# A graph layer with gathered edges: a memset of 128x320 floats on GpSimd in place of the no-operation between gathers

## The chip, the cores and the metric

The kernel runs on one core of one Trainium2 chip. The metric is the device time of one execution in microseconds (us), lower is better. The time before is the median of three runs.

## The reference

A graph has 12500 nodes with 128 features each (`x`, float32) and 412500 directed edges (`src`, `dst`), sorted by destination. Each edge has a gate, a number between 0 and 1, computed from the difference of its two nodes, and the gated differences are summed at the destination:

```python
theta = x[dst] - x[src]
w = sigmoid(relu(theta @ W1 + b1) @ W2 + b2)
agg = segment_sum(w * theta, dst)
indeg = segment_sum(ones, dst)
out = layernorm(x + agg + indeg * (x @ W4 + b4))
```

W1 and W4 are 128x128, W2 is 128x1. Everything is float32.

## The kernel before

**Tables.** `theta @ W1` is the difference of two rows of `x @ W1`, so the kernel first builds a table `z` in DRAM with one row of 256 floats (1 KB) per node: `x @ W1` with the bias, and `x` itself. An edge then needs one row of `z` for its source.

**Parts and blocks.** The edges are cut into 302 parts (`NS`), each for a run of destinations; two parts make a block of at most 96 destinations, 151 blocks in all. The first 26 parts (`PLAIN`) hold 1024 edges and run while the tables and lists are prepared; they are the early parts. Each later part holds up to 1402 edges: 1024 whose source rows are gathered from DRAM, and up to 384 "hot" ones whose source rows TensorE picks out of tables in SBUF, by one-hot matrices (`hot_tiles` on ScalarE, L996 and L998, `hot_products`, L1010, and `hot_rows`, L1051 to L1058, on TensorE).

**The gathers.** `gather(s)` issues the gathers of part `s` on GpSimd: eight indirect DMAs (four for the last part), each of which fetches 128 rows of 1 KB into one of the eight slots of a buffer of `zbuf`; seven such buffers go round. Line L373 is the gather. Ahead of every gather but the very first stands a GpSimd no-operation, `rest` (L367). Manual dependences without semaphores keep the order gather, no-operation, gather. There are 2204 gathers in the later parts, 208 in the early ones.

**What sets the order.** The order of the instructions on TensorE (PE), VectorE (DVE) and ScalarE (ACT) is written out by hand in `part(s)`. For one later part it is about this:

- `logits(s)` on DVE: subtract the gathered half-rows from the products of the destinations `y` (L908), relu times W2 (L913), sum over features (L919); one-hot matrices of the destinations (L888);
- `spread_ahead(s)`: issue the gathers of part `s + 3`. The first of them waits for one semaphore: `paced[s + 3]`, the newest product of `hot_products` or `hot_rows` on PE at that time. The other seven wait for nothing but the order on GpSimd (and for their buffer to be free);
- `add_block` (PE, L1101) sums the weighted rows of the block before; `spread_pair` (PE, L878) and `hot_rows` prepare the next block;
- `open_gate` (ACT, L925) turns the sums into gates; `hot_logits` (DVE, L1068) does the same as `logits` for the hot edges of a block; `weigh` (DVE, L953) and `weigh_rest` (ACT, L960) multiply four of the eight slots each by their gates;
- `normalize` (DVE, L1174 to L1199) is the layernorm of a finished block, whose result goes out by DMA.

`place`, spread over the parts in small steps, prepares the lists of edges for later parts (DVE, L485 to L653; L548 is one of its larger instructions). The core's SyncE (SP) issues most of the plain DMAs.

So GpSimd works a little ahead of the loop of the other engines: the rows of part `s + 3` are asked for while part `s` runs, and how far it runs ahead is bounded by the paced product. The pacing and the call in `spread_ahead` are these lines:

```python
if PLAIN + AHEAD <= s + 3 < NS:
    if s >= PLAIN + 4:
        paced[s + 3] = newest[0]
    gather(s + 3)
```

Of the kernel before, what the change touches and what calls it, by code (L numbers as in the profile page):

```python
# [9 lines left out]
F32 = mybir.dt.float32  # L10
# [10 lines left out]
P = 128  # L21
# [21 lines left out]
PLAIN = FIRST + MORE  # L43
# [36 lines left out]
def gnn_resnorm(  # L80
# [37 lines left out]
    nc = tc.nc  # L118
# [21 lines left out]
    const = ctx.enter_context(tc.tile_pool(name="const", bufs=1))  # L140
# [15 lines left out]
    def set_of(s):  # L156

        s0 = 0 if s < PLAIN else PLAIN + (s - PLAIN) // S2 * S2
        return placed[s0], s - s0
# [42 lines left out]
    def early(n, dtype=F32):  # L202

        a = used_of[0]
        used_of[0] = a + -(-n // (2 if dtype == BF16 else 1))
        assert used_of[0] <= HR * HT * D
        t = tabs_flat[:, a:used_of[0]]
        return t if dtype == F32 else t.bitcast(dtype)
# [49 lines left out]
    rest = early(D)  # L258
# [83 lines left out]
    def slots(s):  # L342
        return [h * J + j for h in range(2) for j in range(pairs(s))]
# [7 lines left out]
    def rows_of(s):  # L351

        if s < NH:
            t = zbuf[s // 2].rearrange("p k d -> p (k d)")[:, (s % 2) * BE:(s % 2 + 1) * BE]
            return t.rearrange("p (k d) -> p k d", d=D)
        return zbuf[(s - NH + NX) % NZ]

    gathers = []
    table_steps = []
    paced = {}  # L360

    def gather(s):

        (src_i, _, _), i = set_of(s)
        for k in slots(s):
            if gathers:
                rest = nc.gpsimd.engine_nop()  # L367
                tc.add_manual_dep(
                    rest.ins, gathers[-1].ins.name,
                    mybir.DependencyInfo(mybir.DependencyClass.NoSync, mybir.DependencyReason.DATA),  # L370
                    reason="between two gathers")
                gathers.append(rest)
            ins = nc.gpsimd.indirect_dma_start(  # L373
                out=rows_of(s)[:, k, :], out_offset=None, in_=z if s >= NH else x,
                in_offset=IndirectOffsetOnAxis(ap=src_i[:, k, i:i + 1], axis=0))
            waits = [(gathers[-1], mybir.DependencyClass.NoSync)] if gathers else []
            at = (s * K + k) * 4 * len(chunks) // (NH * K) - 6
            if s < NH and 0 <= at < len(table_steps):
                waits.append((table_steps[at], mybir.DependencyClass.Sync))
            if k == 0 and s in paced:  # L380
                waits.append((paced[s], mybir.DependencyClass.Sync))
            for other, kind in waits:
                tc.add_manual_dep(
                    ins.ins, other.ins.name,
                    mybir.DependencyInfo(kind, mybir.DependencyReason.DATA), reason="gathers' pace")
            gathers.append(ins)
# [300 lines left out]
    with tc.manual_schedule(engines={SP}), tc.tile_pool(name="work", bufs=2) as wp, tc.tile_pool(  # L687
        name="ps_y", bufs=2, space=bass.MemoryType.PSUM
    ) as ps_y, tc.tile_pool(
        name="ps_l", bufs=1, space=bass.MemoryType.PSUM  # L690
# [526 lines left out]
        def gather_first():  # L1217

            while gathered[0] < AHEAD and (gathered[0] + 1) * len(chunks) <= (len(done) + 1) * NH:
                gather(gathered[0])  # L1220
                gathered[0] += 1
# [70 lines left out]
        def early_part(s):  # L1292
# [15 lines left out]
            if h == 0:  # L1308
# [3 lines left out]
                if b:  # L1312
                    load_u(b - 1)
            gather(s + AHEAD)
            one_hot_w(s)
            logits(s)
# [39 lines left out]
        def spread_ahead(s):  # L1356
# [5 lines that stand above are left out]
# [269 lines left out]
```

## Time and profile before

| | us |
|---|---|
| runs | 3891.53, 3894.61, 3896.5 |
| median of the runs | 3894.61 |
| profiled execution, its own time | 3877.69 |
| its span in the trace | 3875.8 |
| granted TensorE clock, mean of the span | 0.800 |

The profiled execution is 16.9 us (0.4%) under the median of the runs; the prediction starts from its span and says how it stands to the median. The span starts with the tables: in its first tenth the DMAs move up to 265 GB/s in a slice. From about 560 us on to 3838 us the later parts run in the same way, at some 113 GB/s.

How to read the views: a row of a timeline has the start in us, the duration, the engine, the line, the operation, the tile written and the tile read, and in brackets the idle time of the engine ahead of it with what released it. A row of a group has the count, the busy time, the mean in ns and the idle time ahead of its instructions with the releasers. "issue" is idle time in which the engine waited for nothing that the profile shows, "remote" a wait whose releaser the profile cannot name. No-operations are not shown in any view; they lie in the gaps.

### The profile page before, as it was taken

The numbers are of one execution on the slowest core, as the hardware profiler recorded it, in microseconds if no ns is written. First come the engines' busy times: TensorE is split into PE (matmuls) and PEld (weight loads), VectorE is DVE, ScalarE is ACT, GpSimd is POOL, SyncE is SP. The second block draws the span as 40 slices with busy tenths as digits, with TensorE's granted clock in tenths as the row PEclk, the third lists the DMA queues.
The fourth block names the chain that finished last, engine by engine and source line by source line (L and its number), as shares of the span: only waits on it lengthen the run. The fifth ranks groups of instructions, "written<-read, shape, count | busy, mean of one in ns | idle before, by whom it ended". The sixth has DMA issues, their size and how long they took to land.

```text
span 3875.8 us, 56094 instructions
## 1 busy us (share of the span) xinstructions
PE 2445.5 (63%) x15792; PEld 2080.0 (54%) x15792; DVE 2570.0 (66%) x5694; ACT 2136.0 (55%) x5542; POOL 2324.0 (60%) x2421
## 2 busy tenths in 40 slices
PE   6776566666666666666666666656666666666666
PEld 5555455555555555555555555555555555555555
DVE  6445257777775777777657777776577777765555
ACT  5454455555556555555555555555555555555554
POOL 5544436666666666666666666666666666666663
PEclk9786777778778787878888888788878887788887
DMA  7332224444444444444444434444444444444432
GB/s 265 116 106 76 76 76 112 113 110 115 112 113 120 113 113 113 114 112 112 113 119 113 113 112 111 114 111 112 113 113 112 114 113 114 112 112 112 113 108 71
DMA packets 259988, 437.36 MB, mean 113 GB/s; under 512 B 69817, under 2 KB 177800, under 8 KB 258132
## 3 DMA queue, kind: packets, MB, share of 16 engines
q0 software_dynamic: 114752, 312.11, 28.9%
q1 hardware_dynamic: 142946, 115.19, 11.0%
q10 hardware_dynamic: 1970, 6.40, 0.5%
q8 instruction: 127, 2.08, 0.2%
q14 instruction: 193, 1.58, 0.1%
HBM read 406.12 MB, written 27.33 MB: 112 GB/s over the span
## 4 chain that ended last, share of the span: by engine, by line
DVE 29%; another core or an unknown queue 23%; ACT 16%; issue 15%; PE 13%; POOL 2%; DMA 2%; DVEq 0%; SPq 0%; POOLq 0%; ACTq 0%
DVE zbuf L913 5%; DVE zbuf L908 5%; DVE lg L919 4%; DVE hh L1068 4%; ACT wxh L1079 3%; PE pa L1101 3%; ACT wx L960 3%; ACT of L996 2%; PE pd L1010 2%; POOL zbuf L373 2%; ACT of L998 2%; DVE ow L888 2%; ACT xT L1024 1%; DVE ew L555 1%
## 5 line engine op out<-in xcount | busy, mean ns | idle before, releaser
L373 POOL DMA_INDIRECT zbuf<-z,src_i x2204 | 2117.8, 961 | 1323.7 <-issue 497.2
L1010 PE MATMUL pd<-of,tabs 128*128 128x128 f32 (+1 forms) x3392 | 557.0, 330 | 779.3 <-ACT xT L1024 681.1
L1010 PEld LDWEIGHTS pd<-of,tabs 128*128 128x128 f32 x3392 | 523.6, 242 | 799.2 <-ACT xT L1024 696.5
L1101 PE MATMUL pa<-wx,ow 128*96 128x260 f32 (+1 forms) x2620 | 610.2, 386 | 31.1 <-issue 17.9
L908 DVE TENSOR_TENSOR zbuf<-y,zbuf 128x1024 f32<-128x1024 f32 (+1 forms) x276 | 336.3, 1218 | 338.9 <-remote 275.5
L996 ACT ACTIVATE of<-hot_src,nodes 128x512 f32<-128x512 f16 (+2 forms) x424 | 282.0, 701 | 503.8 <-remote 407.8
L1101 PEld LDWEIGHTS pa<-wx,ow 128*96 128x96 f32 x2620 | 419.1, 172 | 172.1 <-issue 40.0
L953 DVE TENSOR_TENSOR wx<-zbuf,fix 128x512 f32<-128x512 f32 x276 | 189.2, 686 | 399.7 <-ACT fix L925 381.5
L878 PE MATMUL y<-y,oh 64*128 64x128 f32 x2204 | 277.4, 362 | 264.2 <-issue 255.7
L878 PEld LDWEIGHTS y<-y,oh 64*128 64x128 f32 x2204 | 222.5, 252 | 309.0 <-issue 288.1
L960 ACT ACTIVATE wx<-zbuf,wx 128x128 f32<-128x128 f32 x1100 | 349.4, 388 | 0.0
L913 DVE SCALAR_TENSOR_TENSOR zbuf<-zbuf,fix 128x1024 f32<-128x1024 f32 (+1 forms) x277 | 336.5, 1215 | 10.6 <-DVE zbuf L908 0.6
L919 DVE TENSOR_REDUCE lg<-zbuf 128x8 f32<-128x1024 f32 (+1 forms) x277 | 334.7, 1209 | 4.7
L1068 DVE SCALAR_TENSOR_TENSOR hh<-px,w_r 128x128 f32<-128x128 f32 x828 | 240.1, 290 | 139.9 <-remote 113.7
L1054 PE MATMUL px<-wni,xT 128*128 128x128 f32 x1656 | 280.8, 321 | 60.3 <-issue 59.9
L1054 PEld LDWEIGHTS px<-wni,xT 128*128 128x128 f32 x1656 | 260.9, 238 | 68.9 <-issue 68.5
L1024 ACT ACTIVATE xT<-pd 128x512 f32<-128x512 f32 (+7 forms) x347 | 132.0, 415 | 297.5 <-remote 253.3
L1101 PE MATMUL pa<-wxh,owh 128*96 128x130 f32 x1656 | 227.3, 277 | 78.5 <-issue 76.9
L1101 PEld LDWEIGHTS pa<-wxh,owh 128*96 128x96 f32 x1656 | 204.5, 164 | 108.8 <-issue 93.3
L925 ACT ACTIVATE fix<-lg,b_c 128x8 f32<-128x8 f32 (+1 forms) x276 | 74.7, 271 | 325.1 <-issue 179.6
L373 POOL DMA_INDIRECT zbuf<-z,src x144 | 137.6, 955 | 144.3 <-ACT wx L943 98.2
L998 ACT ACTIVATE of<-of 128x1024 f32<-128x1024 f32 (+2 forms) x212 | 219.7, 1036 | 6.5
(266 smaller groups left out, 3885.5 us busy)
## 6 DMA issues: line engine op xcount, KB each, us to landing
zbuf<-z,src_i POOLq DMA_INDIRECT x2204
to_all<-off_d SPq DMA_DIRECT2D x276, 112.0 KB
hot_src<-hot_s SPq DMA_DIRECT2D x182, 128.0 KB
z<-zbuf SPq DMA_DIRECT2D x12, 1024.0 KB
xw<-in_x_dram SPq DMA_DIRECT2D x151, 48.0 KB
u<-u_d SPq DMA_DIRECT2D x151, 48.0 KB
out_dram<-o SPq DMA_DIRECT2D x151, 48.0 KB
y<-z SPq DMA_DIRECT2D x294, 24.0 KB
```

The lines of the kernel that those rows point to most:

```text
L373: ins = nc.gpsimd.indirect_dma_start(out=rows_of(s)[:, k, :], out_offset=None, in_=z if s >= NH else x, in_offset=IndirectOffsetOnAxis(ap= ...
L878: nc.tensor.matmul(y[:, j, :], parts[s]["oh"][:, j * P:(j + 1) * P], y_of(s), start=True, stop=True)
L908: nc.vector.tensor_sub(half, yy.to_broadcast([P, 2, n, D]), half)
L913: nc.vector.scalar_tensor_tensor(h[:, at, :], h[:, at, :], 0.0, w2.to_broadcast([P, n, D]), op0=OP.max, op1=OP.mult)
L919: nc.vector.tensor_reduce(lg[:, at, 0], h[:, at, :], AX.X, OP.add)
L960: nc.scalar.activation(wx[:, k, :D], rows_of(s)[:, k, D:], AF.Copy, scale=wx[:, k, D:D + 1])
L996: nc.scalar.activation(of[:, t, :], hot_src[:, i % NU, :w], AF.Abs, bias=nodes[:, t:t + 1])
L998: nc.scalar.activation(of, of, AF.Relu, scale=-1.0, bias=1.0)
L1010: newest[0] = nc.tensor.matmul(to[:, q], tabs[:, g * RG + q, t, :], of[:, t, q], start=t == 0, stop=t == HT - 1)
L1054: nc.tensor.matmul(hot_y(b, h, q), xT[:, h, q * P:(q + 1) * P], wneg, start=False, stop=False, skip_group_check=True)
L1068: nc.vector.scalar_tensor_tensor(h, hot_y(b, *divmod(q, HQ)), 0.0, w2_r, op0=OP.max, op1=OP.mult, accum_out=lg[:, q, :])
L1101: newest[0] = nc.tensor.matmul(to if len(w.shape) == 3 else to[:, 0, :], one, w, start=first and i == 0, stop=last and i == len(terms) - 1)
```

## The change

In the later parts the no-operation ahead of a gather becomes a memset of a tile of 128 partitions by 320 floats, which nothing reads. The early parts keep the no-operation. The dependences around it stay as they are.

```diff
     gathers = []
+    rest_t = const.tile([P, 320], F32, name="rest_t")
     table_steps = []
...
             if gathers:
-                rest = nc.gpsimd.engine_nop()
+                rest = nc.gpsimd.memset(rest_t, 0.0) if s >= PLAIN else nc.gpsimd.engine_nop()
                 tc.add_manual_dep(
                     rest.ins, gathers[-1].ins.name,
                     mybir.DependencyInfo(mybir.DependencyClass.NoSync, mybir.DependencyReason.DATA),
```

2204 no-operations become memsets. The instructions of PE, DVE, ACT, SP and GpSimd stand in the same order in both kernels (4895 on GpSimd in each). Each memset but the first gets a wait for the memset before it, since both write the same tile, and sends a semaphore update; the waits of the gathers are unchanged. The tile takes 1280 bytes more of each partition of SBUF. In the changed kernel every line after L358 has a number larger by one.

## The prediction

> **What bounds the kernel now.** First the page's own head, for the span, and its share of busy time.
>
> ```profile
> span 3875.8 us, 56094 instructions
> PE 2445.5 (63%) x15792; PEld 2080.0 (54%) x15792; DVE 2570.0 (66%) x5694; ACT 2136.0 (55%) x5542; POOL 2324.0 (60%) x2421
> ```
>
> No engine is near full. GpSimd (POOL) is busy for 60%, so it seems to have room for a memset. An average over the span cannot say so: the room has to be next to the gathers. So next the chain of work that ended last, and the costliest group of part 5.
>
> ```profile
> DVE 29%; another core or an unknown queue 23%; ACT 16%; issue 15%; PE 13%; POOL 2%; DMA 2%; DVEq 0%; SPq 0%; POOLq 0%; ACTq 0%
> L373 POOL DMA_INDIRECT zbuf<-z,src_i x2204 | 2117.8, 961 | 1323.7 <-issue 497.2
> ```
>
> POOL holds 2% of the chain. The end is set by the loop of VectorE, ScalarE and TensorE over the parts, with 23% in waits that the profile cannot place ("remote" in the rows below). The gathers run beside that loop. They are 2204 in the later parts, 961 ns each. The next view is the groups of POOL between 700 and 3700 us, where only later parts run, with the busy time of all engines in that stretch.
>
> ```profile
> L373 POOL DMA_INDIRECT zbuf<-z,src_i x1965 | 1889.0, 961 | 1109.6 <-issue 437.3 <-remote 366.9 <-PE px L1058 182.5
> 700.00:3700.00 3000.00, 1877.07 (x12360) 1621.01 (x12360) 2106.24 (x4598) 1691.89 (x4437) 1888.63 (x1965) 0.80 0.42 113
> ```
>
> In the window row the columns are the busy time of PE, PEld, DVE, ACT and POOL, then the granted clock (0.80), the DMA share and GB/s. 1965 gathers in 3000 us is one every 3000/1965 = 1.527 us; a part has eight, so a part takes 12.2 us. The timeline of POOL shows how a part is laid out.
>
> ```profile
> 2002.88 0.94 POOL L373 DMA_INDIRECT zbuf<-z,src_i  x1 [2.23 <-remote]
> 2004.13 0.95 POOL L373 DMA_INDIRECT zbuf<-z,src_i  x1 [0.30 <-issue]
> 2005.38 0.95 POOL L373 DMA_INDIRECT zbuf<-z,src_i  x1 [0.30 <-issue]
> ...
> 2011.63 0.95 POOL L373 DMA_INDIRECT zbuf<-z,src_i  x1 [0.30 <-issue]
> 2014.93 0.94 POOL L373 DMA_INDIRECT zbuf<-z,src_i  x1 [2.35 <-remote]
> ```
>
> Inside a part a gather starts every 1.25 us: 0.95 busy and 0.30 of gap, in which the no-operation and the start of the next gather lie. Then POOL stands for 2.2 to 2.4 us, until the paced product of TensorE lets the next part's first gather go. From 2002.88 to 2014.93 is 12.05 us, the pace of the loop. So the **slack** of POOL is what it would not need if it ran through: mean step 0.961 + 0.305 = 1.266 us, against 1.527 us on offer, which leaves 0.261 us per gather, 2.1 us per part. This number decides the case.
>
> **The change part by part.** It removes 2204 no-operations and adds 2204 memsets of 128x320 floats at the same places of POOL's order. It moves nothing else: the order on every engine stays, the gathers keep their waits. Each memset waits for the one before it, which ended before the gather between them began, so that wait is met; nothing is queued behind it but the next gather. The buffer costs 1280 B per partition and no time.
>
> *Price of a memset.* The later parts show none. The nearest rows stand in the first 2 us of POOL's timeline (start, busy, then what).
>
> ```profile
> 0.25 0.10 POOL L1619 MEMSET const-float32-0.0<- 128x1 f32 x1 [0.25 <-issue]
> 0.28 0.10 POOL L1619 MEMSET const-float32-1.0<- 128x1 f32 x1
> 0.31 0.11 POOL L1619 MEMSET const-bfloat16-1.0<- 128x1 bf16 x1
> ...
> 0.74 0.20 POOL masks.py:197 MEMSET wni<- 128x128 f32 x1 [0.29 <-POOLq L1619]
> 0.99 0.23 POOL L249 IOTA iota_row<- 128x128 f32 x1
> 1.19 0.28 POOL masks.py:199 TENSOR_SCALAR_AFFINE_SELECT wni<-wni 128x128 f32<-128x128 f32 x1
> ```
>
> By duration 127 columns more cost 0.20 - 0.10 = 0.10 us, 0.8 ns a column; 128x320 is then 0.10 + 319 x 0.0008 = 0.36 us. What POOL is held for is the spacing of starts. The memsets of one column start 0.03 apart although each is shown as 0.10, so 320 columns by this row hold POOL for 0.03 + 0.26 = 0.29 us. The 128x128 one is followed 0.25 us later, so by that row 320 columns hold it for 0.25 + 192 x 0.0008 = 0.41 us. I take 0.33, between the two and near the duration. From it goes the no-operation. No view shows one; I count 0.04, about the spacing of the smallest memsets. Net **0.29 us** per gather. The lower end is zero: if the no-operation made up the whole gap of 0.30, 0.29 would merely replace it. The upper end is 0.41: a slow memset and a no-operation that cost nothing.
>
> The Trainium skill bears on which column to believe: "Perfetto Trace Analysis", section GPSIMD Engine Instruction, says that a GpSimd span in a profile is unreliable and that the spacing of starts is to be used. Our rows agree that they differ (0.10 shown, 0.03 apart). It says too that an instruction that reads no tensor has only a point in time, and that these rows contradict, with 0.10 to 0.20 us for memsets. By the span alone the net price would be 0.36 - 0.04 = 0.32 and the sum below 0.03 x 2204 = 66 us larger.
>
> *What of it is hidden.* The first 0.261 us fill the wait ahead of each part's first gather, which the paced product opens. When that is gone, POOL's own pace of 0.961 + 0.305 + 0.29 = 1.556 us per gather, 12.45 us a part, is longer than the loop's 12.2, and every part waits for its rows in the end. Over: (0.29 - 0.261) x 2204 = 64 us. Not all of it is seen, since the gathers are ahead of their use, and that lead is eaten first. The end of the run gives the lead: the last gather, and the first VectorE instruction that takes its rows.
>
> ```profile
> 3837.23 0.95 POOL L373 DMA_INDIRECT zbuf<-z,src_i  x1 [0.30 <-ACT wxh L1072]
> ```
>
> ```profile
> 3856.59 0.68 DVE L908 TENSOR_TENSOR zbuf<-y,zbuf 128x512 f32<-128x512 f32 x1
> ```
>
> That is 19.4 us. I allow 4 us of it for the last gather and its landing, an allowance of mine, so 15 us can be lost unseen. 64 - 15 = **+49 us**.
>
> *What the memset does to others.* VectorE and GpSimd do hold each other up in this kernel: in one part a gather takes 1.64 instead of 0.95 us, and a VectorE instruction of 0.88 us lies over it.
>
> ```profile
> 1429.15 0.94 POOL L373 DMA_INDIRECT zbuf<-z,src_i  x1 [2.43 <-remote]
> 1432.89 1.64 POOL L373 DMA_INDIRECT zbuf<-z,src_i  x1 [0.30 <-DVE wx L953]
> 1438.58 0.95 POOL L373 DMA_INDIRECT zbuf<-z,src_i  x1 [0.30 <-issue]
> 1441.27 0.94 POOL L373 DMA_INDIRECT zbuf<-z,src_i  x1 [1.75 <-PE px L1058]
> ```
>
> ```profile
> 1432.84 0.88 DVE L548 SCALAR_TENSOR_TENSOR ew<-ew 128x702 f32<-128x702 f32 x1
> L1199 DVE TENSOR_SCALAR o<-v,mv,sd 96x128 f32<-96x128 f32 x126 | 44.7, 358 | 1.8 <-issue 1.8
> ```
>
> The gathers' mean of 961 already holds such cases. A memset could be held likewise, or hold VectorE. I cost this at nothing, hidden by the idle third of VectorE (2106 of 3000 us busy); were all 126 of the group L1199 held by half a memset (0.18 us), it would be 23 us.
>
> "SBUF — State Buffer", section Who interferes with whom, of the Trainium skill speaks partly against the change: VectorE in a two-port mode and any GpSimd instruction shut each other out for a whole instruction, while a VectorE instruction with two SBUF inputs contends only with a GpSimd one that reads SBUF. The overlap above, a two-input instruction and a gather, agrees with the second. Memsets would be hit only by the first kind; for that no run here has a price, and 23 us stands for it above.
>
> *Sum.* The profiled execution took 3877.69 us (span 3875.8), 16.9 us (0.4%) under the median of the three timed runs, 3894.61. 3877.7 + 49 = 3926.7, and on the median's footing 3894.6 + 49 = 3944; I say **3942 us**, +1.2%. The bounds: at a net price of 0.261 or less +0; at 0.32 +115; at 0.41 (0.149 x 2204 - 15) +313, 4208 us.
>
> **Rivals.**
>
> *Hidden (same).* The net price stays under 0.261, as it would by the 0.03 spacing (0.29 - 0.04 = 0.25): only the waits of 2.2 to 2.4 us shrink. Time 3895, within 8 us. For it: the nearest memset rows by spacing. Against: a margin of 0.01, and the 0.25 after the 128x128 memset.
>
> *Faster: the pauses let the others proceed.* While gathers flow without a stop, other engines stand. Between 436 and 490 us POOL issued 40 gathers, and the waits of the stretch from 440 to 520 us show this:
>
> ```profile
> 436.00:490.00 54.00, 15.06 (x80) 11.16 (x78) 3.27 (x9) 10.94 (x31) 37.07 (x40) 0.62 0.38 103
> ```
>
> ```profile
> DVE pz L901 <- issue: 48.2, 1, 48.2
> ACT oh L827 <- remote: 45.9, 2, 28.9
> PE pd L824 <- issue: 28.3, 1, 28.3
> ```
>
> ```profile
> DVE zbuf L908 <- remote: 257.2, 54, 6.0
> DVE hh L1068 <- remote: 99.4, 42, 4.1
> ```
>
> (waits: total us, times, longest; the last two are VectorE's from 700 to 3700 us.) If a gap of 0.6 us between two gathers lets TensorE's progress through where 0.30 doesn't, those 357 us shrink: a tenth of them is 36 us there and 36 x 2204/1965 = 40 us in all. I price the case at one to two tenths, -40 to -80, 3835 us in the middle. Against it: POOL's own pace caps it. At a net 0.29 no part can be shorter than 12.45 us; a gain needs a net price clearly under 0.261, and two tenths under 0.22.
>
> *Much slower: the loop is locked to the end of a part's gathers.* If TensorE's product is let through only some 3.3 us after the last gather of a part has started (2011.63 to 2014.93), the wait does not shrink when the burst grows. The burst grows by 7 x 0.29 = 2.0 us, and a part by up to that: 1 to 2 us x 275 parts = +270 to +540 us, 4165 to 4435. It decides from the first tenth of a microsecond. Against it: around 1432.89 the burst is longer by 0.69 us and the wait after it is 1.75 instead of 2.43, so most of the growth was given back.
>
> *A start of its own (slower).* The memset pays a start after a gather, as the 128x128 one waited 0.29 after what precedes it. Then the net is 0.36 + 0.29 = 0.65, and (0.65 - 0.261) x 2204 - 15 = +842 us. Against: instructions of POOL that follow one another without a queue entry between them show 0.0 to 0.05 of gap.
>
> **How the numbers follow.** POOL becomes the bound, by a little to much (net 0.27 to 0.41): 0.45, likeliest 3942. Hidden: 0.17. Faster by pauses: 0.19. Locked: 0.12. A start of its own: 0.07. That the change does not do what it says has no chance to speak of, for the memsets stand in POOL's order. The range goes from 3845 to 4210 us: it takes in the upper bound of the price, the nearer part of the locked case and the smaller gains, and leaves out some 0.07 below and 0.13 above. About 0.2%, 8 us, is what a measurement of this kernel can tell from no change. Faster 0.19, same 0.17, slower 0.45 + 0.12 + 0.07 = 0.64. The likeliest case alone would reach from 3903 to 4208.
>
> **What will show it.** The step inside a part: 1.54 us from gather to gather if the net is 0.29, 1.31 at 0.06, 1.9 with a start of its own. The wait ahead of each part's first gather: about zero if POOL is the bound, with VectorE's L908 waiting for the transfer of `zbuf` instead of "remote", and POOL's share of the chain far above 2%. If the wait stays above 1 us and the time grows all the same, the locked case holds. If "remote" of VectorE falls well below 357 us and the time with it, the pauses helped. The mean of 961 ns should stay within 20 ns, or memset and gather disturb each other in a way that I have not counted. Wrong would make it, first, a memset 0.04 us cheaper than I take it, since 0.029 us over the slack is all that the forecast rests on.

## The result and the profile after

| | before | after |
|---|---|---|
| median, us | 3893.8 | 3831.5 |
| runs, us | 3891.5 to 3896.5 | 3824.6 to 3833.6 |
| profiled execution, own time / span, us | 3877.69 / 3875.8 | 3831.29 / 3829.5 |

The change is **faster** by 1.6%: 0.9837 of before, 95% interval 0.982 to 0.9854. That is under 2%, but clear of no change. By the medians it is 62 us. The two profiles show only 46 of them, since the profile of before is 16 us under its median.

First the page of the changed kernel: its head, the chain of waits and two groups of part 5 (count, busy us, mean ns, idle us ahead).

```profile
span 3829.5 us, 56094 instructions
PE 2580.2 (67%) x15792; PEld 2148.0 (56%) x15792; DVE 2608.5 (68%) x5694; ACT 2132.3 (56%) x5542; POOL 3164.4 (83%) x4625
...
PE 24%; DVE 21%; POOL 19%; issue 13%; ACT 11%; another core or an unknown queue 8%; DMA 4%; SPq 0%; DVEq 0%; POOLq 0%; ACTq 0%
...
L374 POOL DMA_INDIRECT zbuf<-z,src_i x2204 | 2121.2, 962 | 435.1 <-issue 345.2
...
L368 POOL MEMSET rest_t<- 128x320 f32 x2204 | 841.6, 382 | 1.0
```

POOL went from 2% of the chain to 19%, the unplaced waits from 23% to 8%. A gather is not longer (962 ns, 961 before). The next lines are POOL's timeline of the changed kernel, across a part's border: the gather at 2013.63 is the first of part 154.

```profile
2012.14 0.95 POOL L374 DMA_INDIRECT zbuf<-z,src_i  x1 [0.16 <-issue]
2013.09 0.38 POOL L368 MEMSET rest_t<- 128x320 f32 x1
2013.63 0.95 POOL L374 DMA_INDIRECT zbuf<-z,src_i  x1 [0.17 <-issue]
2014.58 0.39 POOL L368 MEMSET rest_t<- 128x320 f32 x1
```

The memset starts when the gather ends, and the gap after it is 0.17 us, not 0.30. So 0.38 us of memset make the step only 0.25 longer: 1.50 instead of 1.25. The wait ahead of a part's first gather is gone but for a few: of 238 parts in the steady stage (from about 700 us on) 10 begin more than 0.1 us later than the step, where in before 232 do. POOL's groups and the busy times of the steady stage follow, and then VectorE's largest waits (total us, times, longest).

```profile
L374 POOL DMA_INDIRECT zbuf<-z,src_i x1950 | 1876.7, 962 | 343.9 <-issue 305.9 <-ACT of L997 6.4 <-ACT wx L961 5.5
L368 POOL MEMSET rest_t<- 128x320 f32 x1949 | 744.1, 382 | 0.9
700.00:3660.00 2960.00, 1961.12 (x12188) 1651.66 (x12190) 2110.36 (x4530) 1664.40 (x4380) 2615.26 (x3899) 0.77 0.42 114
```

```profile
DVE zbuf L909 <- DMA zbuf<-z,src_i: 272.9, 106, 6.0
DVE wx L954 <- ACT fix L926: 158.8, 95, 7.1
DVE hh L1069 <- remote: 126.4, 36, 7.2
```

1950 gathers in 2960 us are one every 1.518 us, 12.14 us a part; busy 0.962, memset 0.382 and idle 0.176 make 1.520. POOL waits for almost nothing any more: it sets the pace. VectorE's "remote" wait at the first instruction of a part (257 us before) has become a wait for the gathered rows (273 us). In before a part took 12.2 us, so all of this stage gives little. The stages show where the rest is. These are the first gathers of part 26 and of part 40 in before, of parts 26 and 40 after, and of the last part after (that of before is at 3833.48).

```profile
436.84 0.94 POOL L373 DMA_INDIRECT zbuf<-z,src_i  x1 [40.14 <-ACT src_i L681]
646.96 0.94 POOL L373 DMA_INDIRECT zbuf<-z,src_i  x1 [3.63 <-PE pd L1010]
3833.48 0.94 POOL L373 DMA_INDIRECT zbuf<-z,src_i  x1 [2.29 <-PE px L1058]
```

```profile
448.23 0.95 POOL L374 DMA_INDIRECT zbuf<-z,src_i  x1 [39.87 <-ACT src_i L682]
625.47 0.95 POOL L374 DMA_INDIRECT zbuf<-z,src_i  x1 [0.17 <-issue]
3796.19 0.95 POOL L374 DMA_INDIRECT zbuf<-z,src_i  x1 [0.17 <-issue]
```

| stage | before, us | after, us | difference |
|---|---|---|---|
| start to part 26 (no memset yet) | 436.8 | 448.2 | +11.4 |
| part 26 to part 40 | 210.1 | 177.2 | -32.9 |
| part 40 to the last part | 3186.5 | 3170.7 | -15.8 |
| last part's first gather to the end | 42.3 | 33.3 | -9.0 |

The sum is -46.3. In the first row nothing is changed yet: in the 18 kept traces, of kernels whose early parts are the same, the first gather of part 26 starts anywhere between 431 and 452 us, and in the profile of before it is an early one. From part 26 on the gain is 58 us, and over half of it lies in 14 of 276 parts, called the first later parts below. There the first seven parts' gathers wait for no product of TensorE. Two lines of TensorE and ScalarE in before show what happens: `pd` (L824) is a product that ScalarE's L827 takes.

```profile
442.85 0.39 PE L824 MATMUL pd<-ident_b,off 128*128 128x128 bf16 x4
473.10 0.59 PE L824 MATMUL pd<-ident_b,off 128*128 128x128 bf16 x4 [28.30 <-issue]
```

```profile
472.27 0.77 ACT L827 ACTIVATE oh<-pd,away,mine 64x512 f32<-64x512 bf16 x1 [28.88 <-remote]
493.48 0.77 ACT L827 ACTIVATE oh<-pd,away,mine 64x512 f32<-64x512 bf16 x1 [17.00 <-remote]
```

The product of 442.85 was done at 443.2, and ScalarE took it at 472.3, 29 us later; the one of 473.1 was taken 20 us later. The ends of products are modelled in this profile, so it shows that ScalarE was released late, but not whether the product or its notice was late. POOL sent 30 gathers without a longer gap from 436.84 to 473.2, and ten more by 490 with gaps of 0.3 to 2.6 us. Late loading of instructions does not explain the stall: from 436 to 485 us the trace has no packet of the instruction queues, and ScalarE and TensorE went on at 472 and 473. The same pair in the changed kernel, and its busy times in the 54 us from its own first gather of part 26 on (the prediction showed 436 to 490 us of before, which start there too):

```profile
456.11 0.40 PE L825 MATMUL pd<-ident_b,off 128*128 128x128 bf16 x4
460.31 0.39 PE L825 MATMUL pd<-ident_b,off 128*128 128x128 bf16 x4
```

```profile
459.30 0.77 ACT L828 ACTIVATE oh<-pd,away,mine 64x512 f32<-64x512 bf16 x1
464.90 0.77 ACT L828 ACTIVATE oh<-pd,away,mine 64x512 f32<-64x512 bf16 x1 [4.17 <-remote]
```

```profile
448.20:502.20 54.00, 41.33 (x237) 33.87 (x236) 17.58 (x37) 28.91 (x70) 47.94 (x72) 0.75 0.48 123
```

Here these products are taken 3 to 4 us after they are done, although POOL runs longer without a stop (its gathers follow one another every 1.50 us from 448 to 530). TensorE has 41 us busy there instead of 15, VectorE 18 instead of 3. Not every stall is gone: the longest waits up to part 40 whose releaser the profile cannot name are 15 us for VectorE and 13 for ScalarE.

### The profile page after: what moved, and what is told of

The parts are those of the page before. It is cut to its first block, busy times and chain, and to the rows that moved or that the text cites. A ratio compares the mean times of both kernels' runs of the same rounds, so it can differ in the third digit from the quotient of the medians.

```text
span 3829.5 us, 56094 instructions
## 1 busy us (share of the span) xinstructions
PE 2580.2 (67%) x15792; PEld 2148.0 (56%) x15792; DVE 2608.5 (68%) x5694; ACT 2132.3 (56%) x5542; POOL 3164.4 (83%) x4625
## 4 chain that ended last, share of the span: by engine, by line
PE 24%; DVE 21%; POOL 19%; issue 13%; ACT 11%; another core or an unknown queue 8%; DMA 4%; SPq 0%; DVEq 0%; POOLq 0%; ACTq 0%
POOL zbuf L374 13%; PE pa L1102 6%; PE pd L1011 5%; POOL rest_t L368 5%; DVE zbuf L909 3%; DVE zbuf L914 3%; DMA zbuf<-z,src_i 3%; DVE lg L920 3%; PE y L879 3%; DVE hh L1069 3%; ACT of L997 2%; ACT wxh L1080 2%; PE px L1055 1%; ACT wx L961 1%
## 5 line engine op out<-in xcount | busy, mean ns | idle before, releaser
L1011 PE MATMUL pd<-of,tabs 128*128 128x128 f32 (+1 forms) x3392 | 673.3, 348 | 699.8 <-ACT xT L1025 539.3
L1011 PEld LDWEIGHTS pd<-of,tabs 128*128 128x128 f32 x3392 | 579.8, 250 | 781.8 <-ACT xT L1025 558.9
L368 POOL MEMSET rest_t<- 128x320 f32 x2204 | 841.6, 382 | 1.0
L909 DVE TENSOR_TENSOR zbuf<-y,zbuf 128x1024 f32<-128x1024 f32 (+1 forms) x276 | 336.7, 1220 | 380.4 <-DMA zbuf<-z,src_i 282.4
L879 PE MATMUL y<-y,oh 64*128 64x128 f32 x2204 | 289.2, 386 | 306.8 <-issue 195.1
L879 PEld LDWEIGHTS y<-y,oh 64*128 64x128 f32 x2204 | 236.9, 274 | 351.9 <-issue 225.3
L1073 ACT ACTIVATE wxh<-lgh,b_c 128x6 f32<-128x6 f32 x138 | 41.9, 304 | 406.9 <-DVE hh L1069 294.6
L1055 PE MATMUL px<-wni,xT 128*128 128x128 f32 x1656 | 262.2, 320 | 0.1
```

What stands on the lines that cost most here:

```text
L368: rest = nc.gpsimd.memset(rest_t, 0.0) if s >= PLAIN else nc.gpsimd.engine_nop()
L879: nc.tensor.matmul(y[:, j, :], parts[s]["oh"][:, j * P:(j + 1) * P], y_of(s), start=True, stop=True)
L909: nc.vector.tensor_sub(half, yy.to_broadcast([P, 2, n, D]), half)
L1011: newest[0] = nc.tensor.matmul(to[:, q], tabs[:, g * RG + q, t, :], of[:, t, q], start=t == 0, stop=t == HT - 1)
L1055: nc.tensor.matmul(hot_y(b, h, q), xT[:, h, q * P:(q + 1) * P], wneg, start=False, stop=False, skip_group_check=True)
```

## The experiments

The kernel before was run beside each group of kernels. It took 3888 us beside the first two groups and 3850 and 3841 beside the last two, so ratios to it are compared, and microseconds only within a group. Ratios have their 95% interval.

**First group: sizes, another kind of pause, and the place.** The theory after the result: pauses between gathers let TensorE's progress through, and with 320 columns POOL sets the pace. The rival: only the first later parts gained, and the loop needs 12.1 us a part whatever the memset.

```diff
-    rest_t = const.tile([P, 320], F32, name="rest_t")
+    rest_t = const.tile([P, 256], F32, name="rest_t")
```

> The memset has 256 columns instead of 320. From the changed kernel's rows (0.38 us for 320 columns, 0.95 for a gather, 0.17 of gap) the step from gather to gather should be about 1.44 us instead of 1.50. Theory (pauses between gathers let TensorE's progress through, and with 320 columns POOL itself sets the pace of the later parts): faster than the changed kernel by up to 0.06 x 2204 = 130 us, if a pause of 0.49 us is still long enough, so 3700 to 3800. Rival (the only gain was in the first later parts, where gathers aren't paced; the loop itself needs 12.1 us a part whatever the memset): within 15 us of 3831.

Measured: 3851.9 us, 0.9924 (0.9894 to 0.9954). Slower than 320 columns by its ratio.

```profile
L374 POOL DMA_INDIRECT zbuf<-z,src_i x1981 | 1905.8, 962 | 446.6 <-issue 311.6 <-remote 72.0 <-PE px L1059 43.4
L368 POOL MEMSET rest_t<- 128x256 f32 x1981 | 650.3, 328 | 1.4
```

(700 to 3700 us.) 1981 gathers are 12.12 us a part. Waits for TensorE are back (72 and 43 us). POOL alone would need 8 x (0.962 + 0.328 + 0.17) = 11.7 us. Here the loop sets the pace, at 12.1, and the theory's 130 us do not come; the rival got the steady stage right in this run. What this kernel loses to 320 columns lies in the first later parts: from part 26 to part 40 it takes 198 us, the change 177 and before 210.

> The memset has 128 columns: about 0.20 us, a pause of 0.37 us between two gathers, hardly more than the 0.30 of the no-operation; step about 1.32. Theory (pauses): either the pause is long enough and the time falls well below that of 256 columns (POOL's own pace would be 10.6 us a part), or it is too short and the waits ahead of each part's first gather return, with a time between the changed kernel's 3831 and before's 3894. Rival (loop of 12.1 us whatever the memset): 3831 within 15.

Measured, with 128 columns: 3878.9 us, 0.9983 (0.9968 to 0.9998). The step is 1.34, the wait ahead of a part's first gather is back (in the median it starts 2.64 us after the gather before it), and almost all of the gain is gone. In this kernel the pause of 0.37 us is too short; the rival's 3831 is out.

```diff
-                rest = nc.gpsimd.memset(rest_t, 0.0) if s >= PLAIN else nc.gpsimd.engine_nop()
-                tc.add_manual_dep(
+                for _ in range(8 if s >= PLAIN else 1):
+                    rest = nc.gpsimd.engine_nop()
+                    tc.add_manual_dep(
...
```

> Eight no-operations instead of the memset in the later parts: nothing is written and no semaphore is sent, POOL only lets time pass. At some 0.03 to 0.04 us each the gap between two gathers should grow from 0.30 to about 0.55 us, the step from 1.25 to about 1.50. Theory (it is the pause): within 20 us of the changed kernel's 3831 and with its step. Rival (the memset itself matters, its writes or its semaphore): like before, 3894, or slower.

Measured: 3896.3 us, 1.0029 (1.0012 to 1.0046). Eight no-operations added only 0.10 us to most gaps, and 18% of the gaps inside a part are over 1 us, as the timeline of POOL shows:

```profile
2003.02 0.95 POOL L374 DMA_INDIRECT zbuf<-z,src_i  x1 [0.40 <-issue]
2004.37 0.95 POOL L374 DMA_INDIRECT zbuf<-z,src_i  x1 [0.40 <-issue]
2006.43 0.95 POOL L374 DMA_INDIRECT zbuf<-z,src_i  x1 [1.11 <-issue]
```

On average the gap inside a part is 0.56 us, as behind the memset, but it is not even. POOL's group from 700 to 3700 us:

```profile
L374 POOL DMA_INDIRECT zbuf<-z,src_i x1945 | 1866.2, 960 | 1134.0 <-issue 874.4 <-remote 93.5 <-ACT wx L961 35.2
```

1945 gathers are 12.34 us a part, a little over before's 12.2. The wait ahead of a part's first gather is mostly gone here too (0.40 us in the median, as inside a part), so that POOL seems to set this pace. In the first later parts the no-operations do what the memset does: from part 26 to part 40 this kernel takes 181 us, the change 177 and before 210. There an idle POOL will do. Whether an even idle pause would do as well as a memset in the steady stage stays open.

```diff
-                rest = nc.gpsimd.memset(rest_t, 0.0) if s >= PLAIN else nc.gpsimd.engine_nop()
+                rest = nc.gpsimd.memset(rest_t, 0.0) if PLAIN <= s < PLAIN + 16 else nc.gpsimd.engine_nop()
```

> The memset of 320 columns in the first 16 later parts alone (parts 26 to 41), the no-operation in all parts after. Between the two profiles the changed kernel is 37 us ahead at the gathers of part 40 (from 15 us behind at part 30 to 22 us ahead at part 40) and gains only 16 us more over the remaining 260 parts. Theory (most of the gain comes from the stage in which gathers run without a paced wait): 3894 - 30 to 45, 3850 to 3865. Rival (the gain is spread over all later parts): 3885 to 3895.

Measured: 3857.4 us, 0.992 (0.9893 to 0.9947), 30 us. As the stage table of the profiles has it: the memset in 16 parts of 276 brings about half of the gain. From part 26 to part 40 this kernel takes 171 us.

**Second group: the two stages apart, and what holds the loop.**

```diff
+            if s + AHEAD >= PLAIN and newest[0] is not None:
+                paced[s + AHEAD] = newest[0]
             gather(s + AHEAD)
...
-                if s >= PLAIN + 4:
-                    paced[s + 3] = newest[0]
+                paced[s + 3] = newest[0]
```

> No memset. The first seven later parts (26 to 32), whose gathers in before wait for no product of TensorE, get the paced wait too: the first gather of each waits for the newest product at that time. In before 30 gathers ran there without a longer gap and DVE and ACT stood for 48 and 29 us. Theory (the gain of the first later parts comes from gathers that no longer run without a stop, and a paced wait is a stop as well): 20 to 40 us faster than before, like the memset in parts 26 to 41 alone (30 faster). Rival (the gain needs a pause between every two gathers): within 10 us of before.

Measured: 3852.8 us, 0.9911 (0.9882 to 0.9939), 36 us, with no memset at all. Two of the longest waits from 436 to 600 us:

```profile
DVE pz L901 <- remote: 16.7, 1, 16.7
ACT oh L827 <- remote: 16.3, 1, 16.3
```

In before these two lines waited for up to 48 and 29 us. The first 16 gathers still run on at 1.25 us; the first stop is a wait of 9.7 us for a product of L1101, which can be the newest one too. From part 26 to part 40 this kernel takes 183 us. In this stage it is not the memset as such that helps, but that the gathers do not run on at a step of 1.25 us.

```diff
         for k in slots(s):
+            if s >= PLAIN and k % 2:
+                continue
             if gathers:
```

> Before with every second gather of the later parts left out, with its no-operation: the rows of those slots stay what an earlier part left there, so the output is not the reference's. All work of the other engines is the same. In the runs so far a later part takes 12.1 to 12.3 us whatever the step of the gathers (1.25 to 1.50). Theory (the flow of gathers holds TensorE's progress back, and that sets the 12.1): a part falls clearly below 12, to 10 to 11 us, 300 to 500 us less in all. Rival (the instructions of PE, DVE and ACT themselves need 12.1 us a part): within 30 us of before.

Measured: 3095.0 us, 0.7959 (0.7934 to 0.7984). In 2300 us of the steady stage stand 973 gathers, four to a part: 9.5 us a part. The window of the steady stage and the chain of waits of this run:

```profile
700.00:3000.00 2300.00, 1729.28 (x12212) 1521.99 (x12210) 2058.43 (x4539) 1664.34 (x4399) 932.96 (x973) 0.85 0.34 91
```

```profile
DVE 49%; ACT 17%; PE 14%; issue 13%; another core or an unknown queue 4%; DMA 1%; POOL 1%; SPq 0%; DVEq 0%; POOLq 0%; ACTq 0%
```

The unplaced waits are down from 23% to 4%, and the instructions of the three engines need no more than 9.5 us. So 2.7 us of the 12.2 in before go with the gathers that were left out. Not all of it can be won with every gather kept: POOL alone needs 8 x 1.266 = 10.1 us for eight. The granted clock is higher as well, 0.85 against 0.80, and TensorE is busy for 7.1 us a part instead of 7.6, so up to 0.5 us may be the clock's. The theory held, the amount was more than expected.

> A memset of 384 columns: 0.38 + 0.06 = 0.44 us, step about 1.56. If POOL sets the pace of the later parts in the changed kernel (8 steps of 1.52 make the 12.14 us of a part), each part gets 8 x 0.06 = 0.48 us longer: 270 x 0.48 = 130 us over the changed kernel, about 3960, 65 slower than before. Rival (the loop of the other engines sets the pace and POOL follows): within 15 us of the changed kernel, 3831.

Measured, with 384 columns: 3934.1 us, 1.0119 (1.0089 to 1.0148), 45 us slower than before, where 65 was expected. POOL's groups from 700 to 3700 us:

```profile
L374 POOL DMA_INDIRECT zbuf<-z,src_i x1908 | 1840.7, 965 | 332.3 <-issue 255.5 <-ACT wx L961 27.3 <-ACT a L1140 11.0
L368 POOL MEMSET rest_t<- 128x384 f32 x1907 | 831.1, 436 | 0.9
```

12.58 us a part, 0.44 more than with 320 columns. POOL sets the pace, as foretold for the change.

```diff
-                rest = nc.gpsimd.memset(rest_t, 0.0) if s >= PLAIN else nc.gpsimd.engine_nop()
+                rest = nc.gpsimd.memset(rest_t, 0.0) if s >= PLAIN + 16 else nc.gpsimd.engine_nop()
```

> The no-operation up to part 41, the memset of 320 columns from part 42 on: the other half of the run that had it in parts 26 to 41 alone and came out 30 us under before. If the two halves add up to the change's 62: 25 to 35 us faster than before. Theory (most of the gain lies in the first later parts): 10 to 30 faster. Rival (the two do not add up, since the backlog of the first parts is what the rest lives on): same as before within 8.

Measured: 3862.2 us, 0.9943 (0.9922 to 0.9965), 26 us. With the other half 0.992 x 0.9943 = 0.986, near the change's 0.984: the two stages add up. In the first later parts this kernel takes 210 us, like before, and shows before's stall again (waits, 436 to 600 us):

```profile
DVE pz L902 <- remote: 48.2, 1, 48.2
ACT oh L828 <- remote: 45.9, 2, 28.2
```

**Third group: is it POOL's work or the gathers, and both remedies together.**

```diff
         for k in slots(s):
+            if s >= PLAIN and k % 2:
+                for _ in range(2):
+                    rest = nc.gpsimd.memset(rest_t, 0.0)
...
+                continue
```

> Every second gather of the later parts is left out as in the run that took 3095 us (its rows stay what an earlier part left, so the output is not the reference's), and in its place stand two memsets of 320 columns, 0.76 us of work for POOL that moves no rows. POOL is then busy 4 x (0.95 + 0.76) = 6.8 us of a part of 9.6, 71%, against 60% in before. Theory (what holds the others back is the flow of gathers, not that POOL works): within 60 us of 3095. Rival (any work of POOL holds them back, by its share of time): most of the loss is back, 3500 to 3900.

Measured: 3092.1 us, 0.804 (0.802 to 0.806). POOL's memsets in the place of gathers cost nothing (POOL, the fifth busy time, has 1652 us here against 933 without them):

```profile
700.00:3000.00 2300.00, 1726.28 (x12179) 1519.31 (x12177) 2059.78 (x4519) 1652.56 (x4384) 1651.64 (x2902) 0.85 0.33 90
```

What holds the others back is the flow of gathers and not that POOL works. These two runs do not tell what of the flow does it: the issuing of a gather, the transfers, or how soon the last rows of a part are there.

```diff
+    rest_t = const.tile([P, 288], F32, name="rest_t")
...
-                rest = nc.gpsimd.engine_nop()
+                rest = nc.gpsimd.memset(rest_t, 0.0) if s >= PLAIN else nc.gpsimd.engine_nop()
```

and the paced wait of the second group.

> The paced wait for all later parts, and a memset of 288 columns in all later parts: step about 1.47, so that POOL's pace of 8 x 1.49 = 11.9 us a part lies a little under the 12.1 of the loop. Theory (in the first later parts either remedy will do; in the rest a memset under the point where POOL sets the pace costs nothing): 3810 to 3835, the same as the changed kernel or up to 20 us under it. Rival (the wait and the pause get in each other's way, as the other sizes came out slower): over 3840.

Measured: 3754.0 us, 0.9755 (0.9732 to 0.9777).

> The paced wait for all later parts, and the change's memset of 320 columns. Theory (both act on the same stage, the first later parts, so their gains do not add): within 15 us of the changed kernel. Rival (they add): 30 us under it, near 3800.

Measured: 3805.2 us, 0.9884 (0.986 to 0.9907).

> The changed kernel itself once more, on the chip of the two runs before it and beside the same runs of before: 3831 within 12, ratio 0.984 within 0.003. If it comes out nearer to 0.99, the distance of the other sizes from it was that of chips, not of kernels.

Measured: 3804.6 us, 0.9883 (0.9863 to 0.9902). The ratio missed the 0.984 expected: beside this group before ran 1% faster, and the change 0.7%. In the steady stage this run has 1981 gathers in 3000 us, 12.12 us a part, as the first time (12.14): what POOL sets is the same. That the loop of before was faster here is inferred from its times alone, since no profile of before was kept in this group. The paced wait adds nothing to 320 columns (from part 26 to part 40 both take 170 us), so both act on the same stage. 288 columns are 1.3% under 320, 8 x 0.026 = 0.21 us a part by the step (1.470 against 1.496), some 56 us over 270 parts, as measured (51). This fits POOL as the bound and leaves the 256 columns of the first group odd.

**Fourth group: 288 and 256 columns, with and without the paced wait.**

> The change with 288 columns instead of 320, no other edit. The run with 288 columns and the paced wait for all parts took 0.9755 of before, the change 0.9883 on the same chip, while 320 columns with that wait were no better than without. Theory (the size alone does it: POOL still never waits, and sets a pace of 8 x 1.49 = 11.9 us a part instead of 12.1): 0.975 to 0.980 of before, and no wait ahead of a part's first gather. Rival (288 columns need the paced first parts to stay clear of the waits, like 256 columns, which gave 0.992 without): 0.988 to 0.993, with waits.

Measured: 3753.1 us, 0.9779 (0.9749 to 0.9809).

```profile
L374 POOL DMA_INDIRECT zbuf<-z,src_i x2010 | 1938.6, 964 | 349.7 <-issue 297.9 <-ACT wx L961 15.5 <-ACT fix L926 7.7
L368 POOL MEMSET rest_t<- 128x288 f32 x2011 | 715.1, 356 | 1.2
```

2010 gathers are 11.94 us a part, and there is no wait for TensorE among POOL's largest. The size alone does it; the rival is out.

> 256 columns once more, beside 288 on one chip. Theory (a pause of 0.49 us is too short to let TensorE's progress through; the waits return): 0.990 to 0.994 of before, 12.1 us a part, slower than 288 columns by 1% or more. Rival (it was that chip; a smaller memset is always faster until it is gone): 0.965 to 0.972, 11.7 us a part.

Measured: 3765.6 us, 0.9807 (0.9783 to 0.9831). Neither value: 11.88 us a part (2020 gathers), not 12.1 and not POOL's own 11.7, with fewer waits than in the first group:

```profile
L374 POOL DMA_INDIRECT zbuf<-z,src_i x2020 | 1944.8, 963 | 395.8 <-issue 321.9 <-remote 34.7 <-PE px L1059 13.8
L368 POOL MEMSET rest_t<- 128x256 f32 x2020 | 663.8, 329 | 0.9
```

Part of the first group's distance seems to have been that group's slower loop. Another part lies in the first later parts: 198 us there, 185 here, 167 with 288 columns. With 256 columns the loop is the bound in both, at 11.9 and at 12.1 us.

> 256 columns and the paced wait for all later parts. Theory (waits return under some 0.5 us of pause whatever the first parts do): within 0.4% of 256 columns without. Rival (what spoils 256 columns is the backlog of the first parts): 0.965 to 0.972 of before.

Measured: 3753.8 us, 0.9779 (0.9753 to 0.9805), with the same 11.88 us a part. In the steady stage the waits return at this size with or without the backlog of the first parts. The theory's 0.4% holds, but the 12 us between the two kernels are not nothing, for their runs do not overlap: from part 26 to part 40 this one takes 167 us and the one without the paced wait 185. So the backlog of the rival is there too, as a smaller part.

> 272 columns and the paced wait for all later parts: step about 1.455. Theory (there is an edge between 256 and 288 columns, above which POOL sets the pace and below which waits return): either 0.970 to 0.975 of before with no waits, 11.8 us a part, or 0.98 to 0.99 with some. Rival (no edge): 0.970 to 0.973.

Measured: 3747.8 us, 0.9757 (0.9733 to 0.9782): 11.87 us a part, with small waits (9 us "remote" in 3000). It is not told apart from 288 columns with the paced wait. Both beat before by 2.4%; 288 columns with the paced wait beat the change by 1.3% in the group where both ran, and 272 columns were not run beside the change.

## Why the prediction was wrong

*Slack.* 0.261 us per gather, from the steady stage. This stood: 384 columns are over it and slower, 320 columns just under.

*Price of the memset.* The duration came out as 0.382, not 0.36, and the price per column as foretold (0.328, 0.382 and 0.436 for 256, 320 and 384 are 0.84 ns each). The net price was the mis-sized term: 0.29 was taken, and the steps say 1.518 - 1.266 = **0.25**. The gap ahead of a gather shrank from 0.30 to 0.17 behind a memset, which the prediction had only as its lower bound, by way of the no-operation. With 0.25 the term (net - slack) x 2204 turns from +64 us to (0.25 - 0.261) x 2204 = -24; the steady stage gave -16. The prediction named this as the first thing that would make it wrong, a memset 0.04 us cheaper than taken. The no-operation counted from it was sized about right: one view does list it, the chain of waits of before, with 0.03 us where 0.04 was counted.

```profile
513.67 0.03 POOLq L367
```

On the Trainium skill's rule in "Perfetto Trace Analysis", section GPSIMD Engine Instruction, that spacing and not duration counts: the runs agree, 0.25 of spacing against 0.38 shown.

*The step that failed: the excess over the slack, "(0.29 - 0.261) x 2204 = 64 us".* Beside its mis-sized term, its count is wrong. The slack of the stage from 700 us on was multiplied by all 2204 gathers, as if the first later parts were like the rest. They are not: their first gathers wait for nothing, so there was no slack to fill and a stall to remove. The prediction quoted that stall (48 us of VectorE, 29 of ScalarE) for the rival and gave that stage no term of its own. It measured -33 us in the profiles and -30 to -36 by two separate edits. A third, the eight no-operations, took 29 us off the same stage in its profile.

*The rival "faster".* It was given 0.19 and 3835 us in the middle, and 3831.5 came out. The direction was right, and the mechanism named, pauses that let the others proceed, fits the runs; that the number came so near is luck. Its price was one to two tenths of 357 us of waits in the steady stage, while over half of the gain lies in the first later parts, which it did not price. It was also capped with POOL's own pace, which binds only in the steady stage; the gain in the first parts had no such cap. In the steady stage the cap held: 257 us of "remote" became 273 us of waiting for rows, and little was gained.

*The rival "hidden".* Its condition came true: a net price of 0.25, under the slack. It got there by another sum, for the memset takes 0.38 and the gap behind it gives back 0.13. Its time, no change within 8 us, did not come, because it too had no term for the first later parts.

*POOL becomes the bound.* Right, with the signs that were named: almost no wait ahead of a part's first gather, L909 waiting for `zbuf`, 19% of the chain. Only it did so at 12.14 us a part, just under before's 12.2, where 12.45 was forecast.

*Lead.* The stretch from the last part's first gather to the end became 9 us shorter, where up to 15 us of lead had been counted as a loss unseen. In both cases rows are asked for nearer to their use.

*Locked.* Fell: with 288 columns and more the waits all but vanish.

*A start of its own.* Fell: the 2204 memsets of the change have 1.0 us of idle time ahead of them in all.

*VectorE held by memsets.* The group that the prediction priced at up to 23 us got longer by 89 ns (358 before), 11 us in 124 instructions of the steady stage. The 103 of them that a memset overlaps took 474 ns, the other 21 took 313. What this cost in time was not measured apart:

```profile
L1200 DVE TENSOR_SCALAR o<-v,mv,sd 96x128 f32<-96x128 f32 x124 | 54.7, 447 | 1.0 <-DMA out_dram<-o 1.0
```

## What to carry to other kernels

Price a change by stages: a slack read in the steady stage says nothing of the stage before it, and a stall of 48 us on one page belongs into the sum as its own term. In this kernel an engine that runs ahead slowed the others by running on without a stop. Before such an engine is given a filler, look how late its neighbours' results are taken up, and try sizes: here 272 to 288 columns, at 11.9 us a part, were better than the 320 of the change at 12.1. Compare sizes within one group of runs, since the time of before varied by 1% between groups, while the step of a full POOL did not (12.14 and 12.12 us a part).

## What the runs showed of the hardware

While GpSimd issued 30 gathers at a step of 1.25 us, a product of TensorE was taken up 29 us after its modelled end, and the next one 20 us after; at a step of 1.50 us the same pair was taken up after 3 to 4 us, though single waits of up to 15 us stayed. With half of the gathers a part takes 9.5 us instead of 12.2, and memsets in the place of the others change nothing. By which path gathers hold this up was not shown: neither the number of rows nor their bytes was varied alone. In the first later parts it need not be a memset: a paced wait (183 us) and eight no-operations (181) do nearly what it does (177, before 210). For the steady stage an even idle pause of 0.55 us was not obtained. The granted clock of TensorE was 0.775 with the change and 0.800 before, and its matmuls of L1010 took 348 ns instead of 330; the kernel got faster all the same. Open too is why 256 columns left the loop at 11.9 us in one group and at 12.1 in the other.
